# Some gather chunks of a two-layer graph network fetched row by row by SP and ScalarE

## The chip, the cores and the metric

The kernel runs on one core of one Trainium2 chip. The metric is the device time in microseconds of one execution, as the median of several runs; lower is better. Beside it stands one execution recorded by the hardware profiler, from which all durations below come.

## The reference

12,500 nodes with 128 features each, 200,000 edges sorted by destination. The edge features are passed in and not used.

```python
h0 = relu(layernorm(x))
deg, wsum = segment_sum(1, dst), segment_sum(edge_weight, dst)
w = edge_weight / maximum(wsum, EPS)[dst]
feat = relu(h0 @ W_pool + b_pool)
neigh = segment_max(feat[src] * w, dst)                 # layer 1, 0 where deg is 0
rst = h0 @ W1_self + neigh @ W1_neigh + b1
h = relu(rst / maximum(norm(rst), EPS))
neigh2 = segment_sum(h[src] * w, dst) / maximum(deg, 1) # layer 2
out = x + relu(h @ W2_self + neigh2 @ W2_neigh + b2)
```

What matters here is `feat[src]` and `h[src]`: for each of 200,000 edges a row of 128 float32 numbers (512 bytes) is read from a table in HBM, once per layer.

## The kernel before

**Tables.** A first stage computes the layernorm and `feat` for all nodes and stores `feat` to HBM as `feat_d` (L373). Layer 1 stores its result `h` to HBM as `h_d` (L486), tile of 128 nodes by tile, and layer 2 gathers from there.

**Groups and chunks.** The edges are cut into 391 groups: `GF` = 390 groups of `G` = 512 edges and a tail of 320. A group has up to four chunks of 128 edges. `gather` (L434 to L441) issues one indirect DMA on GpSimd (POOL) for each chunk (L438): row `srcT[p]` of the table goes to partition p of tile `gt`, of which there are eight (L87). That makes 1,563 gathers a layer.

**Layer 1** is the loop at L548, with one turn per group and the work of several groups in each turn. In turn i: SP loads the row of masks `kt` for group i + 4 (`keep_rows`, L536, one of seven tiles); POOL gathers group i; ScalarE scales each gathered chunk by the edge weight (L561) and TensorE transposes it (L562) into `pm`; VectorE runs a segmented running maximum over the group before (L568 to L577); group i - 2 is transposed back (L605), group i - 4 is placed by a matrix product with a selection matrix (L617), and ScalarE writes group i - 5 into the node array `agg` (L610). The node work of a tile of 128 nodes (`nodes1`) is spread over later turns by `node_stage`; its store of `h` goes through SP. Every second turn `side_step` runs some preparation for layer 2 on VectorE.

**Layer 2** is the loop at L635. In turn i: POOL gathers group i from `h_d`; VectorE builds the weighted selection matrix `s` (L641, L643); TensorE multiplies the four chunks of group i - 1 by it (L660, chunk j = 0 starts the sum); VectorE adds group i - 2 into `agg` (L665). About every fourth turn SP loads a tile of `x` (`xr`, L496, four turns ahead), a tile of nodes is finished (`nodes2`, L499), and SP stores it to the output (L508), one turn after its matrix products. ScalarE has no instruction in this loop.

**Order.** Both layers are in a manual schedule: each engine executes its instructions in the order in which the program writes them, and waits at an instruction until the semaphores that it needs have arrived. SP and ScalarE issue the plain DMAs, POOL the indirect ones. `window_at` (L456) loads eight node numbers into registers at once (L459), and the window in `agg` is then addressed by a register. The general fallback from L683 on isn't run with these inputs.

Of the kernel before, what the change touches and what calls it, by code (L numbers as in the profile page):

```python
# [7 lines left out]
F32 = mybir.dt.float32  # L8
BF16 = mybir.dt.bfloat16
I16 = mybir.dt.int16  # L10
I32 = mybir.dt.int32
AF = mybir.ActivationFunctionType
# [5 lines left out]
P = 128  # L18
# [7 lines left out]
TINY = 1e-12  # L26
PAST = 1 << 20
SLOW_B = 64
BL = 8
XC = 8  # L30

# [2 lines left out]
def gnn_kernel(ctx, tc, x, src, dst, ew, w_pool, b_pool, w1s, w1n, b1, w2s, w2n, b2, out):  # L34
# [396 lines left out]
        t, r, ne, _ = edges_of(g)  # L431
        return t, r, ne, [(j, min(P, ne // 2 - j * P)) for j in range(-(-ne // (2 * P)))]

    def gather(pool, table_d, g):  # L434
        t, r, ne, chunks = edges_of(g)
        gt = pool.tile([P, Q, D], F32, name="gt")
        for j, k in chunks:
            nc.gpsimd.indirect_dma_start(  # L438
                out=gt[:k, j, :], out_offset=None, in_=table_d[:, :],
                in_offset=bass.IndirectOffsetOnAxis(ap=srcT[:k, t, j, r:r + 1], axis=0))  # L440
        return gt  # L441
# [73 lines left out]
    with tc.manual_schedule(), tc.tile_pool(name="ew", bufs=3) as wk, \  # L515
            tc.tile_pool(name="ep", bufs=2, space=PSUM) as ps:
        AHEAD = 4
        jobs = [(due, job(lambda: ps.tile([P, Q, P], F32, name="pq", bufs=1), t)) for due, job, t in background()]

        def side_step():  # L520

            while jobs:
                due, steps = jobs[0]
                if next(steps, jobs) is jobs:
                    jobs.pop(0)
                elif i < due:
                    break

        gts, kts, pms, scs, sels, prs, rws, pas = ({} for _ in range(8))
        turn = turns(6)  # L530
        busy = {}

        def keep_rows(g):
            ne = edges_of(g)[2]
            kts[g] = wk.tile([P, G], BF16, name="kt", bufs=AHEAD + 3)
            nc.sync.dma_start(kts[g][:, :ne], keep_d[g:g + 1, :ne].to_broadcast([P, ne]))  # L536

        def node_stage(k):
            if (i, k) in busy:
                st = busy.pop((i, k))  # L540
                next(st, None)
                if k < 5:
                    busy[i + 1, k + 1] = st

        for g in range(AHEAD):
            keep_rows(g)
        carry = NEG
        for i in range(max(turn) + 6):  # L548
            node_stage(5)
            if i + AHEAD < NG:  # L550
                keep_rows(i + AHEAD)
            if i < NG:
                gts[i] = gather(gp, feat_d, i)

            if i < NG:
                t, r, ne, chunks = edges_of(i)
                gs = wk.tile([P, Q, D], F32, name="gs", bufs=2)
                pms[i] = ps.tile([P, G], F32, name="pm")
                gt = gts.pop(i)
                for j, k in chunks:  # L560
                    nc.scalar.activation(gs[:k, j, :], gt[:k, j, :], AF.Copy, scale=ewT[:k, t, j, r:r + 1])  # L561
                    nc.tensor.transpose(pms[i][:, j * P:j * P + k], gs[:k, j, :], ident[:k, :k])  # L562

            g = i - 1
            if 0 <= g < NG:
                ne = edges_of(g)[2]
                kt, pm = kts.pop(g), pms.pop(g)
                nc.vector.tensor_tensor_scan(pm[:, :ne], kt[:, :ne], pm[:, :ne], carry,  # L568
                                             op0=OP.add, op1=OP.max)
                if g + 1 < NG:  # L570
                    carry = wk.tile([P, 1], F32, name="carry")
                    nc.vector.tensor_copy(carry, pm[:, ne - 1:ne])  # L572
                sc = scs[g] = wk.tile([P, G // 2], F32, name="sc")
                two = pm[:, :ne].rearrange("p (c two) -> p c two", two=2)
                new = kt[:, :ne].bitcast(I16).rearrange("p (c two) -> p c two", two=2)
                nc.vector.tensor_copy(sc[:, :ne // 2], two[:, :, 1])  # L576
                nc.vector.copy_predicated(sc[:, :ne // 2], new[:, :, 1], two[:, :, 0])  # L577
            node_stage(1)
            node_stage(3)
            g = i - 3  # L580
            if 0 <= g < NG:
                t, r, ne, chunks = pairs_of(g)
                sels[g] = wk.tile([P, Q // 2, LW], F32, name="sel")
                for j, k in chunks:
                    nc.vector.tensor_scalar(  # L585
                        sels[g][:k, j, :], cols[:k, 1, :], lastT[:k, t, j, r:r + 1],
                        invT[:k, t, j, r:r + 1], op0=OP.is_equal, op1=OP.mult)

                rws[g] = wk.tile([P, Q // 2, D], F32, name="rows")
                pr = prs.pop(g)  # L590
                for j, k in (((slice(0, Q // 2), P),) if ne == G else chunks):
                    nc.scalar.activation(rws[g][:k, j, :], pr[:k, j, :], AF.Copy)  # L592

            node_stage(4)
            if i in turn:
                n = turn[i]
                st = nodes1(wk, ps, n, agg[:, n * P:(n + 1) * P], True)
                next(st)
                busy[i + 1, 1] = st
            g = i - 2  # L600
            if 0 <= g < NG:
                prs[g] = ps.tile([P, Q // 2, D], F32, name="pr")
                sc = scs.pop(g)
                for j, k in pairs_of(g)[3]:
                    nc.tensor.transpose(prs[g][:k, j, :], sc[:, j * P:j * P + k], ident)  # L605

            g = i - 5
            if 0 <= g < NG:
                at = window_at(mybir.EngineType.Activation, g)
                nc.scalar.activation(agg[:, bass.ds(at, LW)], pas.pop(g), AF.Copy)  # L610
            g = i - 4
            if 0 <= g < NG:
                chunks = pairs_of(g)[3]
                pas[g] = ps.tile([P, LW], F32, name="pa", bufs=1)
                rows, sel = rws.pop(g), sels.pop(g)
                for j, k in chunks:
                    nc.tensor.matmul(pas[g], rows[:k, j, :], sel[:k, j, :], start=j == 0,  # L617
                                     stop=j == len(chunks) - 1)
            node_stage(2)
            if i % 2:  # L620
                side_step()
        assert not busy
        i = NG
        side_step()


    with tc.manual_schedule(), tc.tile_pool(name="ew2", bufs=3) as wk, \
            tc.tile_pool(name="ep2", bufs=3, space=PSUM) as ps:
        iota = ps.tile([P, LW], F32, bufs=1)
        nc.vector.tensor_copy(iota, cols[:, 0, :])  # L630
        nc.vector.memset(agg, 0.0)
        gts, ss, pas, xrs = ({} for _ in range(4))
        turn = turns(3)
        late = None
        for i in range(max(turn) + 2):  # L635
            if i < NG:
                gts[i] = gather(gp, h_d, i)
                t, r, ne, chunks = edges_of(i)
                ss[i] = wk.tile([P, Q, LW], F32, name="s")
                hit = ps.tile([P, Q, LW], F32, name="hit", bufs=1)  # L640
                nc.vector.tensor_tensor(hit, iota[:, None, :].to_broadcast([P, Q, LW]),  # L641
                                        locT[:, t, :, r:r + 1].to_broadcast([P, Q, LW]), OP.is_equal)
                nc.vector.tensor_tensor(ss[i], hit, w2T[:, t, :, r:r + 1].to_broadcast([P, Q, LW]),  # L643
                                        OP.mult)
            if i + 4 in turn:
                xrs[turn[i + 4]] = x_rows(wk, turn[i + 4], 6)
            if late is not None:
                stages(late)
                late = None
            if i in turn:  # L650
                n = turn[i]
                late = nodes2(wk, ps, n, agg[:, n * P:(n + 1) * P], xrs.pop(n))
                next(late)
            g = i - 1
            if 0 <= g < NG:
                chunks = edges_of(g)[3]
                pas[g] = ps.tile([P, LW], F32, name="pa")
                gt, s = gts.pop(g), ss.pop(g)
                for j, k in chunks:
                    nc.tensor.matmul(pas[g], gt[:k, j, :], s[:k, j, :], start=j == 0,  # L660
                                     stop=j == len(chunks) - 1)
            g = i - 2
            if 0 <= g < NG:
                at = window_at(mybir.EngineType.DVE, g)
                nc.vector.tensor_tensor(agg[:, bass.ds(at, LW)], pas.pop(g), agg[:, bass.ds(at, LW)], OP.add)  # L665
        assert late is None
# [118 lines left out]
```

## Time and profile before

| what | value |
|---|---|
| median of 3 runs (lowest to highest) | 4074.36 us (4074.12 to 4080.2) |
| the profiled execution: its own time | 4074.64 us |
| its span, first to last instruction | 4072.9 us |
| POOL busy | 3027.6 us (74%), 3,185 instructions |
| PE busy (matmul / weight load) | 2377.9 us (58%) / 1786.8 us (44%) |
| VectorE busy | 1663.5 us (41%) |
| ScalarE busy | 881.8 us (22%), none of it in layer 2 |
| granted TensorE clock, mean | 0.515 |
| queue of POOL's gathers | 100,032 packets, 205.00 MB |
| queue of SP's and ScalarE's transfers | 126,114 packets, 86.22 MB |
| DMA engines busy, layer 1 / layer 2 | about 0.3 / 0.2 |

How to read it: busy time is work of the engine itself; register work, waiting, and the issuing of DMAs by SP and ScalarE are not in it. The span starts with the first stage (to about 114 us), then come layer 1 (to about 2093 us) and layer 2 (from about 2112 us). In lines of a timeline the columns are start, duration (both us), engine, line of the program, operation, destination and sources, and in brackets the idle time before it and what ended it. SPq and ACTq are the issuing sequencers of SP and ScalarE. In a list of groups, "busy, mean ns | idle before, releaser" follow the count; in a line view three durations are minimum, median and maximum in ns, followed by the first and last start.

### The profile page before, as it was taken

What the parts mean: (1) busy time and instruction counts of PE and PEld (TensorE: products, weight loads), DVE (VectorE), ACT (ScalarE), POOL (GpSimd) and SP (SyncE); (2) the same over time, 40 slices, a digit from 0 to 9 for tenths busy, and PEclk for the clock granted to TensorE, in tenths of its full rate; (3) what the DMA queues carried; (4) which work ended last, traced back from release to release, by engine and by line L of the source; (5) the groups of instructions that cost most, each with busy time, mean ns of one, the idle gap of its engine ahead of it and who ended that gap; (6) DMA issues with size and microseconds to landing.
All of it is one profiled execution on the core that took longest, in us unless ns stands there. A gap on an engine that the chain in (4) does not pass through costs nothing.

```text
span 4072.9 us, 32302 instructions
## 1 busy us (share of the span) xinstructions
PE 2377.9 (58%) x8341; PEld 1786.8 (44%) x8341; DVE 1663.5 (41%) x4587; ACT 881.8 (22%) x2908; POOL 3027.6 (74%) x3185
## 2 busy tenths in 40 slices
PE   6566666666666666666655555555555555555555
PEld 4344444444444444444444444444444444444444
DVE  7566666666666655555551111111111121111111
ACT  6344444444444444444420000000000000000000
POOL 4777777777777777777767777777777777777776
PEclk8555555555555555555555555555555555555555
DMA  5333332333333333333322222222222222222221
GB/s 145 86 82 82 81 81 80 81 80 81 81 82 81 82 82 84 83 84 82 82 58 58 59 61 59 59 60 59 60 59 60 59 60 61 59 60 59 60 59 56
DMA packets 228025, 293.88 MB, mean 72 GB/s; under 512 B 62474, under 2 KB 176649, under 8 KB 227835
## 3 DMA queue, kind: packets, MB, share of 16 engines
q0 software_dynamic: 100032, 205.00, 18.5%
q1 hardware_dynamic: 126114, 86.22, 7.8%
q8 instruction: 71, 1.16, 0.1%
q14 instruction: 120, 0.97, 0.1%
q10 hardware_dynamic: 1688, 0.53, 0.1%
HBM read 271.73 MB, written 19.77 MB: 72 GB/s over the span
## 4 chain that ended last, share of the span: by engine, by line
POOL 40%; DMA 32%; issue 21%; PE 3%; ACT 2%; DVE 1%; SPq 0%; POOLq 0%; ACTq 0%; DVEq 0%
POOL gt L438 40%; DMA gt<-feat_d,srcT 16%; DMA gt<-h_d,srcT 14%; ACT gs L561 2%; PE pm L562 1%; PE pn L466 1%; PE pn L465 1%; DMA bases<-in_dst 1%; ACT agg L610 0%; PE pn L489 0%; ACT hT L491 0%; SPq L133 0%; DVE st L402 0%; DVE fb L369 0%; DVE off L386 0%
## 5 line engine op out<-in xcount | busy, mean ns | idle before, releaser
L438 POOL DMA_INDIRECT gt<-feat_d,srcT x1563 | 1503.1, 962 | 478.9 <-issue 397.2
L438 POOL DMA_INDIRECT gt<-h_d,srcT x1563 | 1474.6, 943 | 494.5 <-issue 405.4
L660 PE MATMUL pa<-s,gt 128*128 128x48 f32 x3126 | 1003.4, 423 | 876.7 <-DMA gt<-h_d,srcT 779.0
L660 PEld LDWEIGHTS pa<-s,gt 128*128 128x128 f32 x3126 | 783.1, 312 | 1099.6 <-DMA gt<-h_d,srcT 859.3
L562 PE MATMUL pm<-ident,gs 128*128 128x128 f32 x1563 | 667.5, 461 | 768.3 <-ACT gs L561 751.1
L561 ACT ACTIVATE gs<-gt,ewT 128x128 f32<-128x128 f32 x1563 | 603.9, 400 | 1039.3 <-DMA gt<-feat_d,srcT 1017.3
L568 DVE TENSOR_TENSOR_SCAN pm<-kt,carry,pm 128x512 f32<-128x512 bf16 x390 | 502.1, 1287 | 747.1 <-PE pm L562 747.0
L562 PEld LDWEIGHTS pm<-ident,gs 128*128 128x128 f32 x1563 | 305.3, 203 | 1083.9 <-ACT gs L561 1073.4
L665 DVE TENSOR_TENSOR agg<-pa,agg 128x48 f32 x391 | 81.5, 208 | 1550.1 <-PE pa L660 1054.9
L617 PEld LDWEIGHTS pa<-sel,rows 128*128 128x128 f32 x1564 | 371.5, 327 | 34.9 <-ACT agg L610 34.1
L617 PE MATMUL pa<-sel,rows 128*128 128x48 f32 x1564 | 375.3, 389 | 0.9 <-ACT agg L610 0.9
L605 PE MATMUL pr<-ident,sc 128*128 128x128 f32 x782 | 245.1, 417 | 0.0
L585 DVE TENSOR_SCALAR sel<-cols,lastT,invT 128x48 f32<-128x48 f32 x782 | 206.0, 322 | 0.0
L577 DVE COPY_PREDICATED sc<-kt,pm 128x256 f32<-128x256 int16 x391 | 173.3, 443 | 13.3
L605 PEld LDWEIGHTS pr<-ident,sc 128*128 128x128 f32 x782 | 169.3, 226 | 0.1
L576 DVE COPY sc<-pm 128x256 f32<-128x256 f32 x391 | 162.2, 415 | 0.0
L643 DVE TENSOR_TENSOR s<-hit,w2T 128x192 f32<-128x192 f32 x391 | 139.8, 358 | 13.5
L592 ACT ACTIVATE rows<-pr 128x256 f32<-128x256 f32 x392 | 142.7, 364 | 1.0 <-PE pr L605 1.0
L641 DVE TENSOR_TENSOR hit<-iota,locT 128x192 f32<-128x192 f32 x391 | 139.2, 356 | 0.1
L610 ACT ACTIVATE agg<-pa 128x48 f32 x391 | 79.8, 204 | 140.2 <-PE pn L466 136.7
L465 PE MATMUL pn<-w_2s,hT 128*128 128x128 f32 x196 | 74.4, 484 | 0.0
L572 DVE COPY carry<-pm 128x1 f32<-128x1 f32 x390 | 61.6, 158 | 13.3
(136 smaller groups left out, 1220.5 us busy)
## 6 DMA issues: line engine op xcount, KB each, us to landing
kt<-keep_d SPq DMA_DIRECT2D x390, 128.0 KB
gt<-feat_d,srcT POOLq DMA_INDIRECT x1563, 2.5
gt<-h_d,srcT POOLq DMA_INDIRECT x1563, 2.5
h_d<-h SPq DMA_DIRECT2D x98, 64.0 KB
xr<-in_x SPq DMA_DIRECT2D x97, 64.0 KB
out<-o SPq DMA_DIRECT2D x97, 64.0 KB
agg<-in_x SPq DMA_DIRECT2D x12, 512.0 KB
feat_d<-fr SPq DMA_DIRECT2D x24, 256.0 KB
```

Source lines behind the costliest of these rows:

```text
L438: nc.gpsimd.indirect_dma_start(out=gt[:k, j, :], out_offset=None, in_=table_d[:, :], in_offset=bass.IndirectOffsetOnAxis(ap=srcT[:k, t, j, ...
L561: nc.scalar.activation(gs[:k, j, :], gt[:k, j, :], AF.Copy, scale=ewT[:k, t, j, r:r + 1])
L562: nc.tensor.transpose(pms[i][:, j * P:j * P + k], gs[:k, j, :], ident[:k, :k])
L568: nc.vector.tensor_tensor_scan(pm[:, :ne], kt[:, :ne], pm[:, :ne], carry, op0=OP.add, op1=OP.max)
L576: nc.vector.tensor_copy(sc[:, :ne // 2], two[:, :, 1])
L577: nc.vector.copy_predicated(sc[:, :ne // 2], new[:, :, 1], two[:, :, 0])
L585: nc.vector.tensor_scalar(sels[g][:k, j, :], cols[:k, 1, :], lastT[:k, t, j, r:r + 1], invT[:k, t, j, r:r + 1], op0=OP.is_equal, op1=OP.mult)
L592: nc.scalar.activation(rws[g][:k, j, :], pr[:k, j, :], AF.Copy)
L605: nc.tensor.transpose(prs[g][:k, j, :], sc[:, j * P:j * P + k], ident)
L617: nc.tensor.matmul(pas[g], rows[:k, j, :], sel[:k, j, :], start=j == 0, stop=j == len(chunks) - 1)
L643: nc.vector.tensor_tensor(ss[i], hit, w2T[:, t, :, r:r + 1].to_broadcast([P, Q, LW]), OP.mult)
L660: nc.tensor.matmul(pas[g], gt[:k, j, :], s[:k, j, :], start=j == 0, stop=j == len(chunks) - 1)
```

## The change

In chosen groups chunk j = 0 isn't gathered by POOL. Its 128 rows come by 128 plain DMAs of one row each, whose source address is a register, into a tile `ga` of its own (two of them); the consumers (the scaling at L561 in layer 1, the matrix product at L660 in layer 2) read `ga` in place of `gt[:, 0]` in these groups. In layer 1 it is every 16th group from 32 on, and SP issues all rows; in layer 2 it is every 7th group from 14 on, and SP and ScalarE issue 64 rows each.

`turn(i)` stands at the head of each turn, ahead of all else that SP does in it. It loads the 128 source indices of a group as a row `ri` (one small SP load, one turn earlier), and then issues the rows in batches of `RB` = 8: eight indices into registers, then eight row DMAs. The 16 batches of a group are spread over turns: two batches a turn in layer 1 (turns g - 16 to g - 9 for group g), four a turn in layer 2 (two on SP, two on ScalarE, in turn; turns g - 7 to g - 4).

```diff
+RB = 8
...
+    class Rows:
+        def __init__(self, pool, table_d, every, first, engines):
+            self.pool, self.table_d, self.every, self.first, self.engines = pool, table_d, every, first, engines
+            self.tiles, self.todo, self.index = {}, [], {}
+
+        def takes(self, g):
+            return g >= self.first and g % self.every == 0 and g < GF
+
+        def tile(self, g):
+            return self.tiles.pop(g)
+
+        def turn(self, i):
+            span = self.every
+            g = i + span
+            if self.takes(g):
+                ga = self.tiles[g] = self.pool.tile([P, D], F32, name="ga", bufs=2)
+                ri = self.index.pop(g)
+                each = P // len(self.engines)
+                self.todo = []
+                for r in range(0, each, RB):
+                    for e, eng in enumerate(self.engines):
+                        self.todo.append((eng, ri, ga, e * each + r))
+                self.step = -(-len(self.todo) // (span - 2))
+            for eng, ri, ga, r in self.todo[:self.step] if self.todo else ():
+                _, at = nc.values_load_multi_w_load_instructions(
+                    ri[0:1, r:r + RB], [eng.engine], min_val=0, max_val=N - 1,
+                    skip_runtime_bounds_check_because="sources of edges are nodes, as the gathers have it")
+                for k in range(RB):
+                    eng.dma_start(ga[r + k:r + k + 1, :], self.table_d[bass.ds(at[k], 1), :])
+            if self.todo:
+                self.todo = self.todo[self.step:]
+            g = i + span + 1
+            if self.takes(g):
+                self.index[g] = self.pool.tile([1, P], I32, name="ri", bufs=1)
+                nc.sync.dma_start(self.index[g], src[None, g * G:g * G + P])
+
+    def gather(pool, table_d, g, byrow=None):
...
         for j, k in chunks:
+            if j == 0 and byrow and byrow.takes(g):
+                continue
             nc.gpsimd.indirect_dma_start(
...
+        byrow = Rows(wk, feat_d, 16, 32, [nc.sync])
         for i in range(max(turn) + 6):
+            byrow.turn(i)
...
-                gts[i] = gather(gp, feat_d, i)
+                gts[i] = gather(gp, feat_d, i, byrow)
...
-                    nc.scalar.activation(gs[:k, j, :], gt[:k, j, :], AF.Copy, scale=ewT[:k, t, j, r:r + 1])
+                    rows_j = byrow.tile(i) if j == 0 and byrow.takes(i) else gt[:k, j, :]
+                    nc.scalar.activation(gs[:k, j, :], rows_j, AF.Copy, scale=ewT[:k, t, j, r:r + 1])
...
+        byrow = Rows(wk, h_d, 7, 14, [nc.sync, nc.scalar])
         for i in range(max(turn) + 2):
+            byrow.turn(i)
             if i < NG:
-                gts[i] = gather(gp, h_d, i)
+                gts[i] = gather(gp, h_d, i, byrow)
...
-                    nc.tensor.matmul(pas[g], gt[:k, j, :], s[:k, j, :], start=j == 0,
+                    rows_j = byrow.tile(g) if j == 0 and byrow.takes(g) else gt[:k, j, :]
+                    nc.tensor.matmul(pas[g], rows_j, s[:k, j, :], start=j == 0,
```

More of the change, by code (lines that the diff above doesn't have):

```diff
@@ L432, in pairs_of @@
         return t, r, ne, [(j, min(P, ne // 2 - j * P)) for j in range(-(-ne // (2 * P)))]
-    def gather(pool, table_d, g):
+    class Rows:
[31 more added lines that the diff above has]
+    def gather(pool, table_d, g, byrow=None):
         t, r, ne, chunks = edges_of(g)
```

## The prediction

> **What bounds the kernel now.** I read the page's chain of waits first, then its costliest groups, to learn which engine sets the pace; the line views of L438 and the timelines, to get that pace; the table by windows, to see whether another engine is close behind it.
>
> ```profile
> POOL 40%; DMA 32%; issue 21%; PE 3%; ACT 2%; DVE 1%; SPq 0%; POOLq 0%; ACTq 0%; DVEq 0%
> L438 POOL DMA_INDIRECT gt<-feat_d,srcT x1563 | 1503.1, 962 | 478.9 <-issue 397.2
> L438 POOL DMA_INDIRECT gt<-h_d,srcT x1563 | 1474.6, 943 | 494.5 <-issue 405.4
> ```
>
> The chain is 93% POOL, the landing of POOL's gathers, and "issue" (POOL waiting for nothing that the profile shows). The two groups are the 1,563 gathers of each layer: 943 to 962 ns busy, and 479 to 495 us of idle time in each layer, a fixed gap behind every one. The timeline of POOL in layer 2 shows that gap whether its record names a landing or not:
>
> ```profile
> 3006.99 0.94 POOL L438 DMA_INDIRECT gt<-h_d,srcT  x1 [0.30 <-issue]
> 3008.23 0.94 POOL L438 DMA_INDIRECT gt<-h_d,srcT  x1 [0.30 <-DMA gt<-h_d,srcT]
> 3009.48 0.94 POOL L438 DMA_INDIRECT gt<-h_d,srcT  x1 [0.30 <-issue]
> 3010.73 0.94 POOL L438 DMA_INDIRECT gt<-h_d,srcT  x1 [0.30 <-issue]
> ```
>
> So the "DMA" share of the chain isn't a wait that binds: POOL issues one gather every 1.25 us of itself. The line view gives first and last start of each layer:
>
> ```profile
> L438 POOL DMA_INDIRECT gt<-feat_d,srcT x1563: 908/944/1966, 114.4 to 2092.7; - x196
> L438 POOL DMA_INDIRECT gt<-h_d,srcT x1563: 903/944/961, 2111.9 to 4061.8; - x196
> ```
>
> Layer 2: (4061.8 - 2111.9) / 1562 = 1.2483 us a gather. Layer 1: (2092.7 - 114.4) / 1562 = 1.2665; some of its gathers are long (up to 1.97 us), while the usual pitch is again 1.249. The span is then 114.4 (head) + 1978.3 + 19.2 (between layers) + 1949.9 + 11.1 (tail) = 4072.9 us. The other engines have room:
>
> ```profile
> 1000.00:2000.00 1000.00, 620.64 (x2270) 444.65 (x2270) 592.90 (x1465) 409.92 (x1391) 757.59 (x796) 0.51 0.32 82
> 3000.00:4000.00 1000.00, 554.52 (x1803) 439.70 (x1803) 192.21 (x701) 0.00 (x0) 755.82 (x802) 0.50 0.21 60
> ```
>
> Columns: PE, PEld, DVE, ACT, POOL, clock, DMA share, GB/s. A group is about 5 us; the fullest engine beside POOL is PE, 62% in layer 1 and 55% in layer 2. ACT has no work in layer 2, and the 16 DMA engines are 21 to 32% busy.
>
> **What the Trainium skill says.** GPSIMD Engine Reference, section "When to use GPSIMD": a DMA that POOL issues has its descriptors generated by two of its cores in software; the 944 ns of a gather agree with a cost on POOL itself. DMA: Bandwidth & Descriptors, section "Issuing engines are not separate DMA queues": all queues share 16 DMA engines, and issuing elsewhere saves only the sequencer's issue time; here issue time is exactly what binds, so that is the coin the change pays in. Same page, "Why a DMA increments its semaphore by 16 and not by 1": a one-row transfer uses one engine, and transfers in flight should each have a semaphore of their own. The trace agrees: the one-row load of 1.2 KB is a single packet, and there are 8 semaphores, shared by SP and ScalarE; the ninth transfer of the program waits for the first:
>
> ```profile
> 2.63 0.45 ACTq L162 DMA_DIRECT2D w_1s<-in_L_gnn_W_self  x1
> 3.83 0.34 ACTq L162 DMA_DIRECT2D w_1n<-in_L_gnn_W_neigh  x1
> ```
>
> Price used below, same page, the table beside "DmaMemcpy, per instruction": 512 cycles in "previous generations"; at the 1.2 GHz that Trainium Kernel Development and Optimization, section "NeuronCore Architecture", gives SyncEngine, an estimate of 0.43 us. The traced one-row issues are shorter, so it serves as the upper end only.
>
> **The change, part by part.**
>
> *Removed.* Layer 1: groups 32, 48, ... 384, which is 23; layer 2: groups 14, 21, ... 385, which is 54. Each loses one of its four gathers: 77 gathers. At POOL's pitch 23 x 1.249 + 54 x 1.2483 = 28.7 + 67.4 = 96.1 us, all of it on the path, as POOL waits for nothing else. (If the layer-1 ones were among the long gathers, some 0.35 us more each, 8 us more.)
>
> *Added: row transfers.* 77 x 128 = 9,856 one-row transfers, in batches of 8: one load of 8 registers, then eight times an address calculation and an issue. Durations:
>
> ```profile
> 46.91 0.24 SPq L125 DMA_DIRECT2D dr<-in_dst  x1
> 47.42 0.27 SPq L120 DMA_DIRECT2D er<-in_edge_weight  x1
> 47.73 0.25 SPq L125 DMA_DIRECT2D er<-in_edge_weight  x1
> ```
>
> and, from the line views of ScalarE's register work,
>
> ```profile
> L459 ACTq TENSOR_LOAD <-bases x49: 540/548/994, 146.4 to 2091.5; - x49
> L610 ACTq FUSED_REGOPS  x391: 37/37/37, 147.3 to 2102.6; - x196
> ```
>
> L125 is one row: 0.24 and 0.25 us; 47.42 + 0.27 to 47.73 shows a gap of about 0.045 us between issues. ScalarE's load of 8 registers takes 0.548 us, and 0.07 more pass before the next register operation (0.037). A batch B = 0.62 + 8 x (0.25 + 0.045 + 0.037) = 3.3 us. No SP or ScalarE issue with an address from a register is in this trace; bounds for an issue: 0.23 (the shortest one-row issue) to 0.43 (the price above; a one-row issue at L117 also took 0.428), so B is 3.1 to 4.7. I take 3.3, because an address in a register changes one operand and the three L125 issues agree.
>
> *Does it fit, layer 2?* Seven groups will take 27 x 1.2483 = 33.7 us (34.95 now). SP must issue 8 batches in that time: 26.4 us, plus an out store and an xr load every fourth group (0.34 + 0.43 + gaps, times 7/4, 1.5 us) and the load of indices (0.3): 28.2 us, 84%. ScalarE issues its 8 batches and nothing else. SP would bind from B = (33.7 - 1.8) / 8 = 3.99, a row pitch of 0.42 us against 0.33 expected.
>
> *Does it fit, the semaphores?* Of 8 in a ring, each row waits until the transfer eight before it has landed. A period has 128 rows + some 5 other transfers, so 133/8 = 16.6 times landing plus wake-up. An xr load of 64 KB lands 1.80 us after issue starts, a store after 1.2 to 1.3 (last semaphore packets in the trace); a gather needs 2.5 (its median), from POOL. A row has 512 bytes; I take 1.3 to 1.8: 22 to 30 us of 33.7. It binds above 2.03 us.
>
> *Layer 1.* 16 groups take 63 x 1.249 = 78.7 us; SP needs 16 x 3.3 + 16 kt loads (0.34 + 0.045) + 4 h stores (0.32 + 0.045) = 60.7 us. In a turn with rows SP spends 2 x 3.3 + 0.5 = 7.1 us of a 4.9 us group, for eight turns, so it falls 17 us back. Behind the rows stand the kt load, four groups ahead, and the h store. SP's waits in the profile
>
> ```profile
> SPq L508 <- DVE o L507: 1866.7, 98, 49.2
> SPq L486 <- DVE sel L585: 907.8, 92, 18.8
> ```
>
> show that SP idles most of both layers; kt rows requested at four groups' distance (20 us) cover the 17 us and what landing remains is covered by the scan running a group behind and by eight gt buffers ahead of it, some 35 us before POOL would feel it. Cost nothing; without that cover, up to 23 x 3 = 70 us.
>
> *Added: waits.* Row tiles are due five groups or more after their last row is issued, so L561 and L660 find them landed; each gets several semaphores to check (0.05 us each on PE by its event instructions), up to 0.4 us in a group where PE has over 2 us idle. On ScalarE in layer 2 only rows are queued behind its waits. The ga slot being refilled was last read a period ago. Bandwidth: 9,856 x 512 B = 5 MB beside 294 MB.
>
> *Sum.* The profiled execution took 4074.64 us (span 4072.9 and 1.7 around it), 0.3 above the median of the runs: 4074.64 - 96.1 = 3978.5; half a microsecond for stray waits: **3979 us**, 2.3% less.
>
> **Rivals.**
> (a) *The semaphore ring becomes the pace in layer 2*: with a row landing at 2.07 us the period is 16.6 x 2.07 = 34.4, 0.7 more than POOL's: 54 x 0.7 = 38, so about 4015. For it: SP and ScalarE share the ring and alternate in it. Against: all small hardware-queue transfers seen land sooner. Anything between 3990 and 4066 belongs here.
> (b) *Slower: SP's issue of rows at 0.43 us.* B = 0.62 + 8 x 0.512 = 4.7; a period of layer 2 takes 8 x 4.7 + 1.8 = 39.5 us against 34.95 now. 54 of them are 2133 us from the layer's start at 2083; with some 20 us behind the last and layer 1's gain spent (16 x 4.7 + 8 = 83 of 78.7 us, less its buffers), about 4260. It is slower than now from a row pitch of (34.95 - 1.8 - 8 x 0.62) / 8 / 8 = 0.44 us. For it: L117's 0.428 and the page's price; against: L125, three times.
> (c) *POOL wasn't the bound, no change*: 4074. No engine near 4.8 us a group is seen: in layer 1, at 199 groups in 1000 us, PE is busy for 3.1 us of one and VectorE for 3.0; in layer 2 PE for 2.8.
>
> **How the numbers follow.** Forecast 3971 to 3990: 0.67; (a) 0.13; (c) 0.03; (b) 0.17. Range: 3971 (long gathers removed) to 4064, leaving out (b) and (c). What this kernel's measurement can tell is about 0.2%: faster 0.80, same 0.03, slower 0.17.
>
> **What would show it.** Right: 1,540 and 1,509 gathers, pitch still 1.25, POOL's idle still "issue", layer 2 shorter by 67 us. SP's one-row issues near 0.25, its register load near 0.55. Wrong: L660 or L561 waiting on ga rows, POOL waiting on PE L660 or ACT L561, SP busy through all of a period.

## The result, and the profile after

The changed kernel takes **4172.11 us** (median of four runs, 4171.96 to 4176.56) beside 4074.63 us of the kernel before in the same session: the ratio is 1.0242, with a 95% interval of 1.023 to 1.0255. It is slower by 2.4%; the prediction had said 2.3% faster. (Beside twelve of the eighteen experiments the kernel before itself took 4727 to 4774 us, for a reason that isn't known; those twelve are given below, but no conclusion is drawn from them.)

The chain of waits of the kernel after, first by engine, then by line:

```profile
SPq 36%; issue 18%; DMA 17%; ACTq 12%; DVE 8%; POOL 4%; PE 4%; ACT 0%; POOLq 0%; DVEq 0%
SPq L466 25%; DMA ga<-h_d 11%; SPq L462 9%; ACTq L466 8%; POOL gt L480 4%; ACTq L462 4%; DVE pm L613 3%; PE pa L708 2%; DMA gt<-h_d,srcT 2%; DMA kt<-keep_d 2%; DMA gt<-feat_d,srcT 1%; DVE sel L630 1%; SPq L578 1%; DVE sc L621 1%; DVE sc L622 1%
```

POOL had 40% of this chain before and now has 4%. SP's sequencer has 36%, nearly all of it on two lines: L466, the issue of one row, and L462, the register load ahead of eight rows. ScalarE's sequencer has 12% on the same two lines, all of it in layer 2. The gathers of POOL (L480 is the L438 of before) in the list of groups and in the line view, where the columns are the shortest, the median and the longest duration and the first and last start:

```profile
L480 POOL DMA_INDIRECT gt<-h_d,srcT x1509 | 1423.6, 943 | 635.6 <-issue 364.2
L480 POOL DMA_INDIRECT gt<-feat_d,srcT x1540 | 1477.0, 959 | 492.1 <-issue 382.4
```

```profile
L480 POOL DMA_INDIRECT gt<-feat_d,srcT x1540: 908/944/1874, 114.0 to 2079.3; - x193
L480 POOL DMA_INDIRECT gt<-h_d,srcT x1509: 903/944/977, 2116.2 to 4138.5; - x189
```

The counts are those that were foreseen and a gather still takes 943 to 959 ns. But POOL's idle time in layer 2 rose from 494.5 to 635.6 us although it has 54 gathers fewer. The starts divide the 97.4 us by which the span grew (4072.9 to 4170.3):

| part of the span | before, us | after, us | difference |
|---|---|---|---|
| head, to the first gather | 114.4 | 114.0 | -0.4 |
| layer 1, first to last gather | 1978.3 | 1965.3 | -13.0 |
| from the last gather to layer 2's first | 19.2 | 36.9 | +17.7 |
| layer 2, first to last gather | 1949.9 | 2022.3 | +72.4 |
| from the last gather to the end | 11.1 | 31.8 | +20.7 |

Layer 2 has 54 groups with rows, so a period, from one such group to the next, is about 2022.3 / 54 = 37.45 us (the loads of index rows are 37.4 us apart on average), where POOL alone would need 33.7. What fills it is seen in the timeline of SP, from one load of an index row (`ri`) past the next:

```profile
3021.70 7.60 SPq L466 DMA_DIRECT2D ga<-h_d  x16
3029.40 0.38 SPq L550 DMA_DIRECT2D out<-o  x1
3029.88 0.23 SPq L472 DMA_DIRECT2D ri<-in_src  x1
3030.16 0.36 SPq L538 DMA_DIRECT2D xr<-in_x  x1
3032.27 7.75 SPq L466 DMA_DIRECT2D ga<-h_d  x16
3040.46 0.38 SPq L550 DMA_DIRECT2D out<-o  x1
3041.82 24.94 SPq L466 DMA_DIRECT2D ga<-h_d  x48
3066.81 0.37 SPq L538 DMA_DIRECT2D xr<-in_x  x1
3067.28 0.38 SPq L550 DMA_DIRECT2D out<-o  x1
3067.76 0.25 SPq L472 DMA_DIRECT2D ri<-in_src  x1
```

From one `ri` load to the next are 3067.76 - 3029.88 = 37.88 us, and in them SP issues its 64 rows (16 + 48) and a handful of other transfers. The pauses between the runs are at most about a register load long (0.98 us), but for one: 1.75 us ahead of 3032.27, where SP waits for the index row to land and then loads from it. SP is full.

ScalarE's queue is as full. Between 2200 and 4100 us its 64 rows take 28.0 us of a period and its 8 register loads 9.4, of which 2.6 are the wait for the index row, which SP loads. In 46 of the 54 groups SP issues the last row, but only 0.4 us after ScalarE's last (median). Which of the two queues sets the pace can't be told from this trace; one of the experiments tells it. POOL stands only once in such a period, and what it then waits for is a buffer that TensorE has not read yet:

```profile
3028.83 0.94 POOL L480 DMA_INDIRECT gt<-h_d,srcT  x1 [0.30 <-issue]
...
3033.11 0.94 POOL L480 DMA_INDIRECT gt<-h_d,srcT  x1 [3.33 <-PE pa L708]
...
3070.75 0.94 POOL L480 DMA_INDIRECT gt<-h_d,srcT  x1 [4.22 <-PE pa L708]
```

The two stalls end 37.6 us apart. TensorE's own wait is for the rows. The first line below, from the list of groups, gives all idle time ahead of the products with rows; the others are from the list of waits (columns: total us, times, longest):

```profile
L708 PE MATMUL pa<-s,ga 128*128 128x48 f32 x108 | 33.9, 414 | 1049.0 <-DMA ga<-h_d 434.0
PE pa L708 <- DMA ga<-h_d: 434.5, 20, 25.5
POOL gt L480 <- PE pa L708: 174.5, 115, 5.3
DVE o L549 <- DMA xr<-in_x: 890.3, 59, 25.1
DVE pm L613 <- DMA kt<-keep_d: 669.6, 122, 7.3
```

Here is the whole route of the lost time: SP late, so rows late, so L708 (the L660 of before) waits, so a `gt` buffer comes free late, so POOL waits. (Of the 1049.0 us only 434 are put down to `ga`; the rest stands under other transfers on the same eight semaphores, `ri`, `xr` and `out`.) The last two lines are other work that stands behind rows in SP's queue: the `xr` loads of layer 2 and the `kt` loads of layer 1, which come late as well. And SP's own waits, which were 1866.7 and 907.8 us for work of VectorE before the change (L508 and L486, now L550 and L528), have shrunk to the stray remains of a queue that runs behind:

```profile
SPq L528 <- DVE sel L630: 94.4, 32, 8.9
...
SPq L462 <- DMA ri<-in_src: 66.3, 75, 1.8
...
SPq L550 <- DVE o L549: 26.3, 7, 12.8
```

Last, what one row costs. The line views of L466 and L462:

```profile
L466 SPq FUSED_REGOPS  x6400: 37/37/51, 187.3 to 4149.3; - x194
...
L466 SPq MOVE ga<-h_d x3456: 29/29/29, 2117.7 to 4149.4; - x192
L466 SPq DMA_DIRECT2D ga<-h_d x3456: 224/228/294, 2117.7 to 4149.4; - x192
...
L466 ACTq DMA_DIRECT2D ga<-h_d x3456: 219/219/537, 2118.0 to 4149.2; - x192
```

```profile
L462 SPq TENSOR_LOAD <-ri x800: 683/779/1027, 186.5 to 4145.6; - x160
L462 ACTq TENSOR_LOAD <-ri x432: 547/827/1013, 2116.9 to 4145.0; - x144
```

A row is three instructions: address calculation 37 ns, a MOVE of 29 ns that the prediction had not listed, and the issue, 228 ns. From the records in the trace the median gaps ahead of the three are 51, 36 and 31 ns. A row that waits for nothing is therefore 0.037 + 0.051 + 0.029 + 0.036 + 0.228 + 0.031 = 0.412 us. The run of 48 rows above agrees: 24.94 us hold 48 rows and 5 register loads; with the load at 0.82 (0.78 and a gap of 0.04) a row is (24.94 - 5 x 0.82) / 48 = 0.43. Over layer 2 (2200 to 4100 us) the records give, for a period of SP: 64 rows at a mean of 0.432, 27.6 us; 8 loads with what precedes them at 0.916, 7.3; `xr`, `out` and `ri` 2.45. The sum is 37.4 us, which is the measured period. It has to be, since every instruction is counted with the gap ahead of it; what matters is how little of it is waiting. With the usual gaps alone SP's own work is 64 x 0.412 + 8 x 0.82, with 2.0 for the other transfers, which makes 34.9 us. So SP doesn't fit into 33.7 us even when nothing holds it up. Counted in the same way, ScalarE's is 33.6 us.

### The profile page after: what moved, and what is told of

The parts are those of the page before. It is cut to its first block, busy times and chain, and to the rows that moved or that the text cites. A ratio compares the mean times of both kernels' runs of the same rounds, so it can differ in the third digit from the quotient of the medians.

```text
span 4170.3 us, 63618 instructions
## 1 busy us (share of the span) xinstructions
PE 1909.8 (46%) x8341; PEld 1700.8 (41%) x8341; DVE 1633.3 (39%) x4587; ACT 821.9 (20%) x2908; POOL 2950.4 (71%) x3108
## 3 DMA queue, kind: packets, MB, share of 16 engines
q0 software_dynamic: 97568, 199.95, 17.3%
## 4 chain that ended last, share of the span: by engine, by line
SPq 36%; issue 18%; DMA 17%; ACTq 12%; DVE 8%; POOL 4%; PE 4%; ACT 0%; POOLq 0%; DVEq 0%
SPq L466 25%; DMA ga<-h_d 11%; SPq L462 9%; ACTq L466 8%; POOL gt L480 4%; ACTq L462 4%; DVE pm L613 3%; PE pa L708 2%; DMA gt<-h_d,srcT 2%; DMA kt<-keep_d 2%; DMA gt<-feat_d,srcT 1%; DVE sel L630 1%; SPq L578 1%; DVE sc L621 1%; DVE sc L622 1%
## 5 line engine op out<-in xcount | busy, mean ns | idle before, releaser
L480 POOL DMA_INDIRECT gt<-h_d,srcT x1509 | 1423.6, 943 | 635.6 <-issue 364.2
L480 POOL DMA_INDIRECT gt<-feat_d,srcT x1540 | 1477.0, 959 | 492.1 <-issue 382.4
L607 PE MATMUL pm<-ident,gs 128*128 128x128 f32 x1563 | 466.2, 420 | 966.2 <-DVE sc L622 454.4
L708 PE MATMUL pa<-s,gt 128*128 128x48 f32 x3018 | 721.1, 412 | 177.5 <-DMA gt<-h_d,srcT 148.3
L708 PEld LDWEIGHTS pa<-s,gt 128*128 128x128 f32 x3018 | 679.5, 329 | 218.7 <-DMA gt<-h_d,srcT 148.0
L606 ACT ACTIVATE gs<-gt,ewT 128x128 f32<-128x128 f32 x1540 | 528.4, 397 | 357.3 <-DMA gt<-feat_d,srcT 346.7
L708 PE MATMUL pa<-s,ga 128*128 128x48 f32 x108 | 33.9, 414 | 1049.0 <-DMA ga<-h_d 434.0
L708 PEld LDWEIGHTS pa<-s,ga 128*128 128x128 f32 x108 | 27.2, 312 | 1056.9 <-issue 946.3
L549 DVE SCALAR_TENSOR_TENSOR o<-o,xr 128x128 f32<-128x128 f32 x98 | 28.6, 292 | 891.7 <-DMA xr<-in_x 890.3
L662 PEld LDWEIGHTS pa<-sel,rows 128*128 128x128 f32 x1564 | 351.0, 310 | 34.5 <-ACT agg L655 33.5
```

What stands on the lines that cost most here:

```text
L480: nc.gpsimd.indirect_dma_start(out=gt[:k, j, :], out_offset=None, in_=table_d[:, :], in_offset=bass.IndirectOffsetOnAxis(ap=srcT[:k, t, j, ...
L606: nc.scalar.activation(gs[:k, j, :], rows_j, AF.Copy, scale=ewT[:k, t, j, r:r + 1])
L708: nc.tensor.matmul(pas[g], rows_j, s[:k, j, :], start=j == 0, stop=j == len(chunks) - 1)
```

## The experiments

**My theory**, after the result: SP's own issue work for a row, with its register load, is longer than a period of POOL allows. **The first rival**: the row transfers themselves are slow, and the ring of semaphores (each row waits until the transfer eight before it has landed) sets the pace. **A second**: SP stands at the head of each batch until the index row has landed, because that load is issued just ahead of it. **A third**: ScalarE's queue, and not SP's, sets the pace.

**Rows without registers** (static_rows_b). The same 9,856 one-row transfers from the same queues on the same semaphores, but each from a fixed row of the table. The kernel leaves out the loads of the node numbers and the address calculation, so it fetches other rows than the reference asks for.

```
-                _, at = nc.values_load_multi_w_load_instructions(
-                    ri[0:1, r:r + RB], [eng.engine], ...)
...
-                    eng.dma_start(ga[r + k:r + k + 1, :], self.table_d[bass.ds(at[k], 1), :])
+                    eng.dma_start(ga[r + k:r + k + 1, :], self.table_d[97 * (r + k):97 * (r + k) + 1, :])
```

> The kernel of static_rows again, since in the first session the kernel before itself took 4771 us in place of 4074. Leaves out the loads of indices into registers and the address calculation: the row transfers have fixed source rows, so the chosen chunks hold other rows than the reference's. Issue theory: an SP row costs 0.28 us, 64 x 0.28 + 2.5 = 20.4 us in a period of 33.7, POOL is the bound, about 3980 us. Ring theory: the period stays at 37 us, about 4170 us.

Measured: 3981.28 us beside 4076.34, ratio 0.977 (0.975 to 0.9789). That is nearly the time that the prediction had given for the change. Its chain and its gathers:

```profile
POOL 48%; issue 31%; DMA 14%; PE 3%; ACT 2%; DVE 1%; SPq 0%; POOLq 0%; ACTq 0%
```

```profile
L477 POOL DMA_INDIRECT gt<-feat_d,srcT x1540: 906/945/2052, 115.4 to 2070.3; - x193
L477 POOL DMA_INDIRECT gt<-h_d,srcT x1509: 904/945/962, 2089.1 to 3974.5; - x189
```

Layer 2 takes 3974.5 - 2089.1 = 1885.4 us, 1.250 us a gather: POOL's pace again. The ring does bind here, in SP's queue, and costs nothing there:

```profile
SPq L463 <- DMA ga<-h_d: 360.9, 1079, 9.0
```

SP now meets a semaphore that isn't free 1,079 times and still ends a period in time, since the ring lets 128 rows through in less than 33.7 us. So the ring hypothesis falls for this number of rows, and what had cost the 4172 us lies in what this kernel left out: register load, address calculation, the row's move, and the wait for the index row. It doesn't yet say which of them. This kernel also reads the same 128 rows again and again, so it could be that these land sooner than scattered ones. They don't: ScalarE's rows in layer 2 have a DMA queue of their own, with one packet of 512 bytes and one of 4 bytes for each row, and the second ends 0.91 us after the start of the issue in the changed kernel and 0.94 us here (medians).

**The index row two turns earlier** (ri_early_b).

```
-            g = i + span + 1
+            g = i + span + 3
```

> The kernel of ri_early again, for the same reason. As the change, with the index row loaded two turns earlier. Issue theory: SP loses 0.85 us of waiting in a period, 54 x 0.85 = 46 us: about 4125 us. If ScalarE or the ring were the pace, or the wait only moves: 4165 to 4175 us.

Measured: 4156.32 beside 4076.34, ratio 1.0197 (1.0177 to 1.0217), between the two expectations. The line view shows that it is no test of what it was meant for:

```profile
L480 POOL DMA_INDIRECT gt<-h_d,srcT x1509: 899/944/1048, 2103.3 to 4122.5; - x189
```

Layer 2 takes 2019.2 us, 3.1 less than in the changed kernel. In the program the load moved by two turns of the loop, but a period's rows are all issued in its first turns, and between the old and the new place SP has no row to issue: the load at 3015.13 us is followed by one `xr` load, and then by the register load at 3016.85 that waits for it. Nothing else was put between them. Of the 15.8 us gained, 12.9 lie ahead of layer 2's first gather (2103.3, not 2116.2): in layer 1, which takes 1951.3 us here and 1965.3 in the changed kernel, the earlier load does help.

**Sixteen registers a load** (rb16_d): half as many loads, on SP and on ScalarE, each of twice the registers.

```
-RB = 8
+RB = 16
```

> The kernel of rb16 again, for the same reason: the change with 16 registers a load in place of 8, nothing else. Issue theory: 4040 to 4070 us. If row pitch and ring were all: over 4150 us.

Measured: 4079.38 beside 4076.55, ratio 1.0008 (0.9998 to 1.0017): 92.7 us less than the changed kernel, by one constant, though 9 us above the range expected. The load and the gathers of layer 2:

```profile
L462 SPq TENSOR_LOAD <-ri x400: 1130/1168/1572, 186.5 to 4053.0; - x134
```

```profile
L480 POOL DMA_INDIRECT gt<-h_d,srcT x1509: 902/947/1041, 2084.2 to 4050.9; - x189
```

A load of 16 takes 1.168 us, where two of 8 take 2 x 0.779 = 1.558; with the gap of the load that is saved, that is 4 x (1.558 - 1.168 + 0.04) = 1.7 us a period. Layer 2 became 2022.3 - 1966.7 = 55.6 us shorter, 1.03 a period. The rest went mostly to the ring: what SP waits ahead of its row issues grew from some 0.65 to 1.25 us a period. SP's own work, without waits, would be 34.9 - 1.7 = 33.2 us here and just fit; with the waits for the ring, for the index row (1.0 us) and some smaller ones the period is 36.4 us and remains above POOL's 33.7. Layer 2's first gather moved from 2116.2 to 2084.2, since SP ends layer 1 without a backlog: that is 27.7 us earlier than in the kernel before (2111.9), the 28.7 which the prediction had counted for layer 1. The cost of the loads is thereby shown: a change that touches nothing else of the queues' work brings the time back to that of the kernel before.

**And the index row truly earlier** (rb16_early2_b): as before it, and in layer 2 the row of indices is loaded six turns ahead of its first use, into two tiles instead of one, so that the last 32 rows that SP issues for the group before lie between the load and its first use on SP (3041.44 and 3060.78 us in one period).

```
-            g = i + span + 1
+            g = i + span + self.lead
...
-                self.index[g] = self.pool.tile([1, P], I32, name="ri", bufs=1)
+                self.index[g] = self.pool.tile([1, P], I32, name="ri", bufs=self.kept)
...
-        byrow = Rows(wk, h_d, 7, 14, [nc.sync, nc.scalar])
+        byrow = Rows(wk, h_d, 7, 14, [nc.sync, nc.scalar], 6, 2)
```

> The kernel of rb16_early2 again: every 16th and every 7th group, 16 registers a load, the index row of layer 2 loaded before the last rows of the group ahead, into the second of two tiles. Issue theory: a period of 36.4 becomes 35.4, 54 us less than rb16_d's 4079: about 4025 us. If the ring of semaphores takes up what issue gives back: 4050 to 4080 us.

Measured: 4027.1 beside 4074.7, ratio 0.9881 (0.9865 to 0.9898).

```profile
L481 POOL DMA_INDIRECT gt<-h_d,srcT x1509: 899/944/1052, 2081.4 to 3998.9; - x189
```

Layer 2 takes 1917.5 us, 35.5 a period, 49.2 us less than with the later index row; the ring hasn't taken it back. This is the test that ri_early_b was meant to be: the wait for the index row's landing is 0.9 us of every period, beside the two terms above. (SP's gap ahead of a register load, 0.29 us on average in rb16_d, is 0.045 here, its usual length.) The period is still some 1.8 us above POOL's pace. SP's own work without waits is 64 x 0.412 + 4 x 1.26 + 2.0 = 33.4 us, which would fit; 1.1 us of what is left stands ahead of the row issues, where SP waits for the ring. So close to the limit the ring does cost time.

The trace also settles the third rival. With the index row early ScalarE runs ahead: in 53 of 54 groups it issues its last row before SP does, in the median 17.3 us before, and it then waits for the next index row. So SP, and not ScalarE, sets the pace of layer 2 here. In the changed kernel, too, it was ScalarE that stood longer for the index row, 2.6 us of a period against SP's 0.9.

**Fewer rows** (rb16_18_8_b): the same, with rows in every eighth group of layer 2 from 16 on (47 groups), and every eighteenth of layer 1 from 36 on (20 groups), so that a period of POOL becomes 31 gathers, 38.7 us, for the same rows.

```
-        byrow = Rows(wk, feat_d, 16, 32, [nc.sync])
+        byrow = Rows(wk, feat_d, 18, 36, [nc.sync])
...
-        byrow = Rows(wk, h_d, 7, 14, [nc.sync, nc.scalar])
+        byrow = Rows(wk, h_d, 8, 16, [nc.sync, nc.scalar], 6, 2)
```

> The kernel of rb16_18_8 again, since the kernel before took 4727 us in that session. 16 registers a load, the index row of layer 2 early and in two tiles, every 18th group of layer 1 from 36 (20 gathers fewer) and every 8th of layer 2 from 16 (47 fewer). Issue theory: SP needs 35 of 38.7 us in layer 2 and 76 of 88.7 in layer 1, POOL is the bound: 4074.6 - 84 = 3991 us, faster than both kernels. If SP still binds: 4040 us or more.

Measured: 3989.83 beside 4076.89, ratio 0.9788 (0.9771 to 0.9804). It beats both kernels. Its chain (which could be followed back over layer 2 alone, so that the shares add up to 47%), gathers, and SP's wait:

```profile
POOL 25%; issue 17%; DMA 5%; PE 0%; POOLq 0%; DVE 0%
```

```profile
L481 POOL DMA_INDIRECT gt<-feat_d,srcT x1543: 909/945/1952, 114.2 to 2064.2; - x193
L481 POOL DMA_INDIRECT gt<-h_d,srcT x1516: 901/945/961, 2082.9 to 3975.3; - x190
```

```profile
SPq L551 <- DVE o L550: 238.7, 52, 19.2
```

POOL's pitch in layer 2 is (3975.3 - 2082.9) / 1515 = 1.249 us, SP idles again (for `o` alone 238.7 us, 26.3 in the changed kernel), and 67 gathers removed are worth 87 us: 67 x 1.249 = 83.7, and some 3 us more in layer 1 (1978.3 us became 1949.9, which is 28.4 for 20 gathers), as if some of the gathers removed there had been long ones. With SP inside its period, the prediction's price of a removed gather is right.

**Layer 2 alone** (l2_only_c): `Rows(wk, feat_d, 16, 1 << 20, [nc.sync])`, so that no group of layer 1 takes rows.

> The kernel of l2_only again, for the same reason: the change in layer 2 alone. Issue theory: layer 1 and the gap as before, layer 2 and the tail as after: 4168 us. If the backlog of layer 1 is what slows layer 2: under 4130 us.

Measured: 4180.19 beside 4076.55, ratio 1.0254 (1.0234 to 1.0275).

```profile
L480 POOL DMA_INDIRECT gt<-feat_d,srcT x1563: 908/944/2037, 113.8 to 2092.9; - x196
L480 POOL DMA_INDIRECT gt<-h_d,srcT x1509: 903/944/1043, 2112.2 to 4142.9; - x189
```

Layer 1 and the gap of 19.3 us behind it are those of the kernel before; layer 2 takes 2030.7 us, 80.8 more than before. All of the loss is layer 2's, with its tail. What the part in layer 1 is worth can't be had from the difference to the changed kernel (4180.19 - 4172.11 = 8 us): the intervals of the two ratios overlap, and the 8 us lie in layer 2 (2030.7 us against 2022.3), whose rows are the same in both; why is open. By the table of starts, layer 1 with the gap behind it became 4.7 us longer in the changed kernel, where 28.7 us less were counted.

**What couldn't be compared.** Beside the other twelve runs the kernel before took 4771.24, 4726.86, 4727.84, 4774.27 and 4767.45 us. Their ratios don't carry over to 4075 us: the one edit of sixteen registers a load gives 1.0008 beside 4076.55 us and 1.406 beside 4727.84. Here are the runs, with what was expected of each, by the kernel before that ran beside them. Of most the edit is told above, and the same edit was measured again where the kernel before took about 4075 us.

Beside 4771.24 us: rows without registers, 4820.97 us;

> Leaves out the loads of indices into registers and the address calculation: the row transfers have fixed source rows, so the chosen chunks hold other rows than the reference's. Same number of row transfers, same ring of semaphores. Issue theory (SP's own instructions set the pace: 0.43 us a row and 0.9 us a register load): an SP row costs 0.228 + 0.05 = 0.28 us, 64 x 0.28 + 2.5 = 20.4 us in a period of 33.7, so POOL is the bound again, 4074.6 - 96 = about 3980 us. Ring theory (a transfer waits for the one eight before it, landing 37.45 / 16.6 = 2.26 us): the period stays at 37 us, about 4170 us.

the index row two turns earlier, 6744.89 us;

> As the change, but the index row is loaded two turns earlier, so its landing (0.85 us of SP's wait and 2.6 of ScalarE's in a period of 37.45) is covered. Issue theory: SP is the pace and loses 0.85 us a period, 54 x 0.85 = 46 us: about 4125 us. If ScalarE or the ring were the pace, or the wait only moves: 4165 to 4175 us.

layer 2 alone, 5924.1 us;

> The change in layer 2 alone; layer 1 gathers everything on POOL as before. Issue theory: layer 1 and the gap behind it as before (1978 and 19 us), layer 2 and the tail as after the change (2022 and 32 us): 4160 to 4170 us. If the backlog of layer 1 were what slows layer 2: under 4130 us.

and SP alone at half the rate in layer 2, `Rows(wk, h_d, 14, 28, [nc.sync])` with no rows in layer 1, 5705.69 us.

> Layer 1 as before the change; in layer 2 every 14th group from 28 on, all 128 rows from SP, none from ScalarE, 26 gathers fewer. SP's work per seven groups is that of the change, the ring of semaphores is used half as much. Issue theory: 16 batches of 4.37 us + 4.9 for its other transfers = 75 us for 14 groups, against 69.9 before and 68.7 at POOL's pace: 26 x 5 = 130 us slower than before less what the buffers cover, 4160 to 4200 us. Ring theory: eight semaphores for one issuer, reuse after 3.4 us, no wait; SP needs 57 of 68.7 us, 4074.6 - 26 x 1.25 = 4042 us.

Beside 4726.86 us: layer 1 alone, `Rows(wk, h_d, 7, 1 << 20, [nc.sync, nc.scalar])`, 5551.46 us;

> The change in layer 1 alone, every 16th group; layer 2 gathers everything on POOL. Issue theory: SP is as full as in the change (80 us of work in 16 groups that POOL could do in 78.7), so layer 1 with the gap behind it is as in the change, 2002 us against 1997.5: about 4079 us. If layer 1 alone pays: 4074.6 - 28.7 = 4046 us.

layer 2 alone, 5873.31 us;

> The kernel of l2_only again on a chip at the usual speed: the change in layer 2 alone. Issue theory: layer 1 and the gap as before, layer 2 and the tail as after: 4074.6 + 72.4 + 20.7 = 4168 us. If the backlog of layer 1 is what slows layer 2: under 4130 us.

sixteen registers a load, 6649.47 us;

> The change with 16 registers a load in place of 8, so half as many loads. A load of 1 took 0.467 us and of 8 0.78 us, so one of 16 is put at 1.14. Issue theory: SP saves 8 x 0.82 - 4 x 1.18 = 1.8 us of 37.45 in a period of layer 2 (54 x 1.8 = 97 us) and 3.7 of 80 us in 16 groups of layer 1, which falls back to POOL's pace (31 us with the gap): 4040 to 4070 us. If row pitch and ring were all: over 4150 us.

fewer rows, 6108.27 us.

> 16 registers a load, the index row of layer 2 loaded before the last rows of the group ahead of it and kept in two tiles, and fewer chunks: every 18th group of layer 1 from 36 (20) and every 8th of layer 2 from 16 (47). Issue theory: SP needs 35 of 38.7 us in layer 2 and some 76 of 88.7 in layer 1, so POOL is the bound in both and the 67 gathers are gained: 4074.6 - 84 = 3991 us, faster than both kernels. If SP still binds: 4040 us or more.

Sixteen registers a load again, 6644.47 us beside 4727.84,

> The kernel of rb16 again, for the same reason: the change with 16 registers a load in place of 8, nothing else. Issue theory: SP saves 1.8 us of 37.45 in a period of layer 2 (97 us) and 3.7 of 80 us in 16 groups of layer 1, which falls back to POOL's pace (31 us with the gap): 4040 to 4070 us. If row pitch and ring were all: over 4150 us.

and 6718.02 us beside 4774.27.

> The kernel of rb16 again, for the same reason: the change with 16 registers a load in place of 8, nothing else. Issue theory: 4040 to 4070 us. If row pitch and ring were all: over 4150 us.

Beside 4767.45 us: layer 1 alone, 5598.02 us,

> The kernel of l1_only again: the change in layer 1 alone. Issue theory: SP as full as in the change, layer 1 with the gap behind it as there, 2002 us against 1997.5: about 4079 us. From the difference of the change (1.0242) and its layer-2 part alone (1.0254): about 4070 us. If layer 1 alone pays: 4046 us.

and sixteen registers with the index row truly earlier, 6706.9 us.

> As rb16_d (every 16th and every 7th group, 16 registers a load), and the index row of layer 2 loaded before the last rows of the group ahead, into the second of two tiles, so that SP does not stand 1.0 us and ScalarE 2.9 us for its landing. Issue theory: a period of 36.4 becomes 35.4, 54 us less: about 4025 us. If the ring of semaphores takes up what issue gives back, as in half of rb16_d's gain: 4050 to 4080 us.

Two edits were never measured elsewhere: layer 1 alone (ratios 1.1746 and 1.1736) and sp_only_14 (1.1962). For a kernel before of 4075 us both remain open.

## Why the prediction was wrong

**Right.** POOL bounds the kernel before, at 1.25 us a gather, and a removed gather is worth that: static_rows_b and rb16_18_8_b end where this puts them. The counts, the unchanged pitch, the issue on SP (0.228 us where 0.25 was taken, the lower bound being 0.23) and the ring (it isn't the pace at 128 rows in 33.7 us; static_rows_b) are right.

**The step that failed** is "Does it fit, layer 2?": SP's need of 28.2 us a period was 37.4. The sum is right in its form and in its threshold, and three of its terms are too small. A batch measured 0.916 + 8 x 0.432 = 4.37 us; that is within the prediction's own bounds of 3.1 to 4.7, above its threshold of 3.99, and far from the 3.3 that it took:

| term, us a period of layer 2 | predicted | measured |
|---|---|---|
| 64 rows | 64 x 0.332 = 21.2 | 64 x 0.432 = 27.6 |
| 8 register loads | 8 x 0.62 = 5.0 | 8 x 0.916 = 7.3 |
| `xr`, `out`, `ri` | 1.8 | 2.45 |
| sum | 28.0 | 37.4 |

*The row.* The issue was priced, and the path to it wasn't. Per row, the issue is 0.022 us shorter than taken; a MOVE adds 0.029; the three gaps together are 0.118 and not 0.045, 0.073 more; some 0.02 are gaps and issues longer than usual, half of it ahead of the issue, where SP waits for the ring. Together that is the 0.10 us a row. The prediction bounded "an issue" by 0.23 and 0.43, and reasoned that an address in a register changes one operand. It changes the number of instructions. And each instruction has its own gap, of 31 to 51 ns, as long as the address calculation or the MOVE itself. The trace of before showed such gaps (0.07 after ScalarE's load); only one of them was counted per row. The prediction itself had found that SP binds from a row pitch of 0.42 and loses from 0.44; without any waiting the row is at 0.412, and with the true load the threshold is lower still, (33.7 - 2.45 - 8 x 0.82) / 64 = 0.386.

*The load.* ScalarE's load of 8 registers in the kernel before (0.548 us) was used for SP. SP's takes 0.779, and ScalarE's own for rows now 0.827. Of 0.916 us a load, 0.82 are the load and its usual gap, and the rest, about 0.8 us in a period, mostly the wait for the index row at the first load of a period. rb16_d and rb16_early2_b show both: 55.6 us for half the loads, 49.2 for the index row.

*The index row* stood in the sum as 0.3 us of issue. It was named nowhere as a wait, though it is loaded in the turn ahead of its first use and has only an `xr` load between.

**The layer-1 step**: SP's 60.7 us in 78.7 were some 76 of its own work (128 x 0.412 + 16 x 0.82, and 10.0 for the other transfers), for the same reasons, and with its waits (2.9 us ahead of the `h` stores, for VectorE; 0.9 for the index row) the `ri` loads of layer 1 lie 82.0 us apart. The buffers hid this for three quarters of the layer; from 1587 us on POOL stood seven times, for 2.6 to 3.5 us each. So the layer gained 13.0 us where 28.7 were counted, and gave 17.7 back between the layers, since SP arrives there with a queue of late work; with sixteen registers a load that gap is 19.3 us again (2064.9 to 2084.2). "Cost nothing" failed there; the bound of 70 us without the cover was kept.

**The tail**, +20.7 us, wasn't in the sum; it is the same backlog at the end of layer 2. The last row is issued at 4149.4 us, 10.9 us after the last gather, and the six groups from that one on can only then be finished.

**The rivals.** Rival (b) is the one that came true: SP as the pace, `PE L708` waiting for rows, POOL for PE, all as its signs were written. Its price was put on the wrong term (an issue of 0.43 us, where it is a row of 0.43 with an issue of 0.228), and its total was 4260, because its row was 0.43 + 0.045 + 0.037 = 0.51. Its 39.5 us a period against 37.4 measured are 54 x 2.1 = 113 us. That its period came so near is partly luck: an issue 0.2 us too long stood in for the MOVE, the gaps and the longer load that it left out. The upper price from the Trainium skill (DMA: Bandwidth & Descriptors, the table beside "DmaMemcpy, per instruction": 512 cycles, at 1.2 GHz an estimate of 0.43 us) isn't what an issue costs here: 0.219 to 0.228 us were measured on both engines. Rival (a), the ring, falls by static_rows_b as the pace; it shows up as about a microsecond of waits in a period, and it holds back rb16_d (with the index row) and rb16_early2_b, where SP's own work alone would fit. Rival (c) falls with the two faster kernels.

What stays open: what more semaphores in the ring would give, since no run has them; what layer 1 does alone; and why layer 2 took 8 us more in l2_only_c.

The Trainium skill's remark in the same page, section "Issuing engines are not separate DMA queues", that issuing from several engines only saves the time on the sequencer, "which is usually small relative to the DMA itself", has its counterpart here. A row of 512 bytes lands 0.91 us after the start of its issue and costs SP's sequencer 0.43 us, about half of that. But landings overlap in the ring and the sequencer's times add up, so the sequencer was the bound, while static_rows_b, with as many transfers, shows that the landing was not.

## What to carry to other kernels

When work is moved to an idle queue, price the whole loop of one item on that queue: every instruction that it becomes, address work and moves included, and a gap of 30 to 50 ns for each; a bound on the longest instruction alone is no bound. Write down the period of the engine that is being relieved beside the need of the one that is loaded, and take seriously a threshold that lies only about a quarter above the estimate: here 0.42 against 0.33 was called room, and it decided the sign. If the loaded queue just fails to fit, give it fewer items before giving up the idea, since above the threshold each period pays and below it the gain comes back (rb16_18_8_b).

## What the runs showed of the hardware

- A load of registers from SBUF on SP takes 0.467 us for one register (L731, one instance), 0.779 for 8 and 1.168 for 16: 0.045 to 0.05 us for each register more, on a base of 0.42. So few large loads are better than many small ones. On ScalarE the median is 0.827 for 8 and 1.295 for 16, while the load of 8 registers in the kernel before took 0.548; what makes this difference wasn't tried.
- An issue with its address in a register is hardly longer than one with a fixed address: 0.228 us on SP beside 0.215 in static_rows_b, 0.219 beside 0.212 on ScalarE. The first row issue after a register load takes longer, 0.453 us on ScalarE and 0.266 on SP (medians in the changed kernel).
- A ring of 8 semaphores passed 128 one-row transfers and some five others in under 33.7 us, so a row's issue, landing and wake-up take less than 8 x 33.7 / 133 = 2.03 us on average (static_rows_b). The last packet of a row ends 0.91 us after the start of its issue (median of ScalarE's rows in the changed kernel).
